# Graph attention on one core: 48 gathers added behind the batches, and one buffer for gathered rows less

## The chip, the cores and the metric

The kernel runs on one core of a Trainium2 chip. The metric is the device time of one execution in microseconds (us); the time before is the median of three runs. The profile is that of one execution of its own.

## What is computed

One graph-attention layer with a residual and a layer norm. There are N = 6250 nodes with D = 128 features, and E = 206250 edges, sorted by destination; 8 heads of 16 features each.

```python
Qh = (h @ WQ).reshape(N, H, D)
Kh = (h @ WK).reshape(N, H, D)
Vh = (h @ WV).reshape(N, H, D)
Eh = (edge_attr @ WE).reshape(-1, H, D)
src, dst = (edge_index[0], edge_index[1])
score = jnp.einsum('ehd,ehd,ehd->eh', Kh[src], Qh[dst], Eh) * inv_sqrt_d
score = jnp.exp(jnp.clip(score, -5.0, 5.0))
msg = Vh[src] * score[:, :, None]
wV = jax.ops.segment_sum(msg, dst, num_segments=N)
Z = jax.ops.segment_sum(score, dst, num_segments=N)
h_out = wV / (Z[:, :, None] + 1e-06)
x = layernorm(x + h_out)
```

## The kernel before

Edges are cut into 1612 tiles of 128, and the tiles into batches of four (smaller ones at the very end), about 405 in all. A table `kv` in DRAM holds the K and V rows of all nodes, 256 floats or 1 KB a node. The rows of an edge's source node are fetched by an indirect DMA on GpSimd's queue, the *gather* of line 314: 128 rows of 1 KB for each tile, four gathers for a batch, into one of GB = 17 buffers `kvrows` of 4 KB a partition. The first XB = 12 batches gather from `x`, since `kv` is still being written. The last tile has only 42 edges; its gather is cut to 64 rows.

The loop over batches is unrolled and in an order written out by hand. Step b does, in the order of the code: loads of edge features (`ea`), of relative destinations (`relb`) and of query windows (`qw`) on SyncE's queue; the four gathers of batch b (`gather(b)`); on TensorE the transposes of batch b-1 (`turn`, line 373, into `pps`), the expansion of the queries of batch b (`stage_a`, line 354, into `qps`) and its edge projection (line 358, into `eps`); the sums over finished windows of destinations (`finish`, line 401); on VectorE the product of batch b-2 with its gathered K rows (`stage_b`, line 379, `kq`) and its reduction (line 382), the messages of batch b-3 from its gathered V rows (`messages`, line 413), the one-hot matrices of batch b+2 (lines 340 and 344), and the product `eq` of batch b (line 365). ScalarE evicts `qps` (line 356), takes the exponentials (391, 393), and copies finished sums. TensorE adds up the messages by destination (`stage_c`, line 431, `agg`). Now and then `q_rows` (lines 258 to 265) makes another block of query rows: a matmul, a cast on ScalarE, a difference on VectorE, a cast and a difference again, and a store.

The gathers are tied to TensorE's pace. From batch LOCK = 16 on, the first gather of batch b waits for the matmul of line 354 of batch b - lag(b), where lag falls from 12 by one every four batches and is 1 from batch 60 on:

```python
def lag(b):
    return max(STEP, 12 - (b - LOCK) // 4)
```

A gather that takes a used buffer also waits until VectorE's line 413 has read the batch that had it.

The lines that the prediction uses: 314 (gathers), 354 (`qps`), 358 (`eps`), 365 (`eq`), 373 (`pps`), 379 (`kq`), 413 (`msg`), 431 (`agg`), 258, 261 and 262 (`q_rows`).

Of the kernel before, what the change touches and what calls it, by code (L numbers as in the profile page):

```python
# [8 lines left out]
F32 = mybir.dt.float32  # L9
# [6 lines left out]
P = 128  # L16
N, E, D, H, DH = 6250, 206250, 128, 8, 16
# [7 lines left out]
MW = D + H  # L25
B = 4
CH = 8
GB = 17
XB = 12
LOCK = XB + 4  # L30
STEP = 1
TAIL = 8
HEAD = 132
NG = (NT + G - 1) // G
# [14 lines left out]
def cut_batches():  # L49
    out, t = [], 0  # L50
    while t < NT:
        k = B
        if t >= NT - TAIL:
            k = 2 if NT - t > 3 else 1
        out.append(range(t, t + k))
        t += k
    return out
# [23 lines left out]
def edge_attention(ctx: ExitStack, tc: tile.TileContext, x, xT, srcT, dstT, dstB, dst0, bnd, lo, eaT,  # L81
                   wq, wkv, we, out, kv, qtab, qs, relD):
    nc = tc.nc
# [25 lines left out]
    def src_col(t):  # L109
        return src_sb[0][:, t:t + 1] if t < C0 else src_sb[1][:, t - C0:t - C0 + 1]  # L110

    with ExitStack() as fast:
        ip = fast.enter_context(tc.tile_pool(name="init", bufs=1))
        nc.scalar.dma_start(dst_sb[:, :C0], dstT[:, :C0])
        lo_sb = ip.tile([P, NG], I32, name="lo_sb")
        nc.scalar.dma_start(lo_sb, lo)
        io_i = ip.tile([P, 3 * P], I32, name="io_i")
# [84 lines left out]

        gp = fast.enter_context(tc.tile_pool(name="gather", bufs=GB))
        ep = fast.enter_context(tc.tile_pool(name="edges", bufs=EB))
# [42 lines left out]
        batches = cut_batches()  # L247
# [55 lines left out]
        def lag(b):  # L303

            return max(STEP, 12 - (b - LOCK) // 4)

        def gather(b):
            rows, f = (x, D) if b < XB else (kv, 2 * D)
            g = gp.tile([P, B, 2 * D], F32, name="kvrows")
            for i, t in enumerate(batches[b]):  # L310
                k = min(P, (E - t * P + 63) // 64 * 64)
                if k < P:
                    nc.vector.memset(g[k:, i, :], 0.0)
                ins = nc.gpsimd.indirect_dma_start(  # L314
                    out=g[:k, i, :f], out_offset=None, in_=rows,
                    in_offset=bass.IndirectOffsetOnAxis(ap=src_col(t)[:k], axis=0))
                if i == 0 and b >= LOCK:
                    tc.add_manual_dep(ins.ins, expanded[b - lag(b)].ins.name,
                                      mybir.DependencyInfo(mybir.DependencyClass.Sync, mybir.DependencyReason.DATA),
                                      reason="gathers keep to TensorE's pace")  # L320
            return g

        def project(g, n):
# [94 lines left out]
        def stage_c(b):  # L418
            n, g, oh, m = st8.pop(b)
            for i in range(n):  # L420
# [18 lines left out]
                elif last:  # L439
# [3 lines left out]
                    if k[1] == 0 and k[0] > 0:  # L443
                        ready.append(k[0] - 1)

        gathered = {b: gather(b) for b in range(min(XB, len(batches)))}
        for b0 in range(0, NB, KB):
            table(b0)
# [15 lines left out]
        for b in range(nbat + 4):  # L464
# [6 lines left out]
            if b < nbat:  # L471
                load_chunk(batches[b][0] // CH + EB - 3)
                load_rel(batches[b][0] // RC + 1)
                load_q(batches[b][0] // WT + QLOOK)
                g = gathered.pop(b) if b in gathered else gather(b)
                if b == min(XB, nbat - 1):
                    late_loads()
                if b == min(XB + 8, nbat - 1):
                    relative(C0, NT)
                if b == 14:  # L480
                    from_window(1)
                if b == 0:
                    for i in range(AHEAD):
                        stage_0(i)
                if b > 0:
                    turn(b - 1)
                stage_a(b, g)
            elif b == nbat:
                turn(b - 1)
# [178 lines left out]
```

## Time and profile before

| what | value |
|---|---|
| median of three runs | 2424.27 us (2415.33 to 2429.15) |
| the profiled execution | 2430.0 us, span 2428.1 us |
| mean granted TensorE clock | 0.81 |
| TensorE matmuls, busy | 1539.8 us, 63% |
| VectorE, busy | 1577.4 us, 65% |
| ScalarE, busy | 458.9 us, 19% |
| GpSimd, busy | 1534.0 us, 63% |
| DMA moved | 398.16 MB, mean 164 GB/s |
| gathers from `kv` | 1564, mean 951 ns on GpSimd |

How to read it: an engine's busy time counts its instructions and leaves out the time in which its sequencer issues, waits or branches. A gather's time on GpSimd is that of making its descriptors, not that of the transfer. Of each group of instructions a view gives the busy time, the mean time of one, and the idle time of the engine just before, with what ended it: "issue" stands where nothing that the profile shows was waited for, "remote" where the releaser is not among the instructions shown. In a timeline each line has the start, the length, the engine, the line of the code and the operation, and in brackets the idle time before it. The records of matmuls start when they are recorded to start, while their ends are modelled.

### The profile page before, as it was taken

Reading aid. Unit: us, or ns where it says so; the run is one execution under the profiler, and the core shown is the slowest. Engines: PE = TensorE matmul, PEld = TensorE weight load, DVE = VectorE, ACT = ScalarE, POOL = GpSimd, SP = SyncE. Lnnn points to the kernel's source line nnn. Section 1 sums busy time; section 2 is a strip of 40 time slices with the busy share of each in tenths; the row PEclk is TensorE's granted clock in tenths of the full one; section 3 lists DMA queues with packets and bytes.
Section 4 is the critical chain, followed back from the end, with each engine's and each line's share of the span. In section 5 each row is a group of like instructions: output and inputs, shape, how many; then the busy total and the mean of one; then the engine's idle time right before and its main releaser. Section 6 shows DMA issues by size and latency. Waiting matters only on the chain.

```text
span 2428.1 us, 24930 instructions
## 1 busy us (share of the span) xinstructions
PE 1539.8 (63%) x6880; PEld 1086.0 (45%) x6880; DVE 1577.4 (65%) x3779; ACT 458.9 (19%) x1572; POOL 1534.0 (63%) x1619
## 2 busy tenths in 40 slices
PE   3587666666665666657666666666666656656665
PEld 2365444444444444444444444444444444444444
DVE  1368778666766666667667666666666667666766
ACT  0232122111111111111111111111111111111111
POOL 7346565666666666666666666666666666666664
PEclk6898898887878888778877878788778788887887
DMA  5645555556554555556456554655555556554642
GB/s 176 201 144 174 179 156 178 165 150 185 170 166 148 168 177 156 164 152 196 147 157 196 160 156 149 184 168 151 169 162 178 147 155 196 157 156 146 197 150 71
DMA packets 178482, 398.16 MB, mean 164 GB/s; under 512 B 61756, under 2 KB 87526, under 8 KB 178336
## 3 DMA queue, kind: packets, MB, share of 16 engines
q0 software_dynamic: 76592, 208.18, 29.4%
q1 hardware_dynamic: 100604, 187.38, 25.2%
q8 instruction: 57, 0.93, 0.2%
q10 hardware_dynamic: 1140, 0.93, 0.1%
q14 instruction: 89, 0.73, 0.1%
HBM read 381.54 MB, written 14.81 MB: 163 GB/s over the span
## 4 chain that ended last, share of the span: by engine, by line
PE 34%; another core or an unknown queue 23%; DVE 19%; issue 16%; ACT 4%; DMA 2%; POOL 1%; DVEq 1%; SPq 0%; ACTq 0%; POOLq 0%
PE agg L431 10%; PE eps L358 10%; PE pps L373 7%; DVE sc L382 4%; DVE kq L379 4%; DVE eq L365 3%; PE qps L354 3%; ACT qT L356 2%; DVE msg L413 2%; PE finps L401 2%; POOL kvrows L314 1%; DVE onehot L340 1%; DVE onehotT L344 1%; DMA kvrows<-kv,src 1%
## 5 line engine op out<-in xcount | busy, mean ns | idle before, releaser
L314 POOL DMA_INDIRECT kvrows<-kv,src x1564 | 1487.1, 951 | 862.3 <-issue 385.6
L431 PEld LDWEIGHTS agg<-msg,onehot 128*128 128x128 f32 x3224 | 516.7, 230 | 664.3 <-issue 520.9
L431 PE MATMUL agg<-msg,onehot 128*128 128x136 f32 x3224 | 560.5, 326 | 352.8 <-DVE msg L413 137.2
L373 PE MATMUL pps<-shift,eq 128*128 128x128 f32 x1612 | 320.5, 332 | 419.6 <-DVE eq L365 238.5
L365 DVE TENSOR_TENSOR eq<-qT,eps 128x512 f32<-128x512 f32 x406 | 276.4, 681 | 476.2 <-ACT qT L356 210.9
L358 PE MATMUL eps<-ea,we_sb 128*128 128x512 f32 (+1 forms) x812 | 528.2, 738 | 16.8 <-issue 13.4
L373 PEld LDWEIGHTS pps<-shift,eq 128*128 128x128 f32 x1612 | 221.4, 168 | 477.4 <-DVE eq L365 282.4
L356 ACT COPY qT<-qps 128x512 f32<-128x512 f32 x406 | 236.8, 583 | 1048.5 <-remote 428.8
L379 DVE TENSOR_TENSOR kq<-kvrows,pps 128x512 f32<-128x512 f32 x406 | 274.8, 677 | 12.1 <-remote 3.5
L413 DVE TENSOR_TENSOR msg<-kvrows,bank 128x512 f32<-128x512 f32 x406 | 274.6, 676 | 9.8 <-ACT bank L391 4.3
L382 DVE TENSOR_REDUCE sc<-kq 128x32 f32<-128x512 f32 x406 | 276.0, 680 | 7.3
L340 DVE TENSOR_TENSOR onehot<-bank,dst_sb 128x512 f32<-128x512 f32 x406 | 275.8, 680 | 0.0
L358 PEld LDWEIGHTS eps<-ea,we_sb 128*128 128x128 f32 x812 | 192.1, 238 | 50.0 <-issue 14.6
L354 PE MATMUL qps<-onehotT,qw 126*128 126x512 bf16 x406 | 187.3, 461 | 0.9 <-ACT qT L356 0.9
L344 DVE TENSOR_SCALAR onehotT<-relb,node 126x512 bf16<-126x512 bf16 x406 | 147.0, 363 | 16.7 <-remote 11.2
L391 ACT ACTIVATE bank<-sc 128x32 f32<-128x32 f32 x406 | 83.0, 204 | 257.2 <-DVE onehot L340 139.8
L401 PEld LDWEIGHTS finps<-sum,shift 128*128 128x128 f32 x478 | 73.1, 215 | 62.4 <-issue 33.9
L401 PE MATMUL finps<-sum,shift 128*128 128x136 f32 x478 | 75.8, 307 | 30.9 <-ACT sum L441 26.2
L262 DVE TENSOR_TENSOR qr<-qrows,qst 128x128 f32<-128x128 f32 (+1 forms) x49 | 14.2, 289 | 116.8 <-ACT qst L261 104.4
L393 ACT ACTIVATE msg<-sc 128x32 f32<-128x32 f32 x406 | 88.0, 217 | 0.0
L385 DVE TENSOR_SCALAR sc<-sc 128x32 f32<-128x32 f32 x406 | 79.2, 195 | 7.3
L441 ACT COPY sum<-agg 128x136 f32<-128x136 f32 x146 | 39.3, 269 | 236.2 <-remote 100.7
(66 smaller groups left out, 525.9 us busy)
## 6 DMA issues: line engine op xcount, KB each, us to landing
ea<-eaT SPq DMA_DIRECT2D x201, 512.0 KB
relb<-relD SPq DMA_DIRECT2D x100, 504.0 KB
kvrows<-kv,src POOLq DMA_INDIRECT x1564
qw<-qs SPq DMA_DIRECT2D x202, 31.5 KB
kv<-kvst SPq DMA_DIRECT2D x12, 512.0 KB
qs<-qst SPq DMA_DIRECT2D x48, 96.0 KB
xb<-x SPq DMA_DIRECT2D x48, 64.0 KB
out<-h SPq DMA_DIRECT2D x48, 64.0 KB
```

What stands on the lines that cost most here:

```text
L314: ins = nc.gpsimd.indirect_dma_start(out=g[:k, i, :f], out_offset=None, in_=rows, in_offset=bass.IndirectOffsetOnAxis(ap=src_col(t)[:k], a ...
L340: nc.vector.tensor_tensor(oh[:, :n], iota_p[:, None, :].to_broadcast([P, n, P]), rel[:, t0:t0 + n, None].to_broadcast([P, n, P]), op=ALU.i ...
L354: expanded[b] = nc.tensor.matmul(pq[:, :n * P], loaded[t0 // WT], ohT[:, :n * P], start=True, stop=True)
L356: nc.scalar.copy(qT[:, :n * P], pq[:, :n * P])
L358: nc.tensor.matmul(pe[:, :n * P], we_sb, ea_tiles(t0, n), start=True, stop=True)
L365: nc.vector.tensor_tensor(eq[:, :n * P], qT[:, :n * P], pe[:, :n * P], op=ALU.mult)
L373: nc.tensor.transpose(pp[:, i, :], eq[:, i * P:i * P + P], ident)
L379: nc.vector.tensor_tensor(t1[:, :n], g[:, :n, :D], pp[:, :n], op=ALU.mult)
L382: nc.vector.tensor_reduce(sc[:, :n], t1[:, :n].rearrange("p b (h d) -> p b h d", h=H), axis=AX.X, op=ALU.add)
L401: nc.tensor.matmul(ps, shift[:, P - s:2 * P - s], sums[k], start=i == 0, stop=stop and i == len(parts) - 1)
L413: nc.vector.tensor_tensor(m[:, :n, :D].rearrange("p b (h d) -> p b h d", h=H), g[:, :n, D:].rearrange("p b (h d) -> p b h d", h=H), exp_p[ ...
L431: nc.tensor.matmul(aggs[k], oh[:, i, :], m[:, i, :], start=first and not final, stop=last)
```

## The change

Behind the gathers of each batch from 100 to 147 one more gather is issued on GpSimd's queue. It reads rows of `kv` by the first r indices of the batch's first tile, with r from a list of twelve values, each used in four batches running: 124, 126, 127, 120, 112, 96, 64, 32, 16, 8, 4, 2. All 48 write the first r partitions of one tile `short` (1 KB a partition), which nothing reads. The buffers for gathered rows become 16 instead of 17, which makes room for that tile.

```diff
-GB = 17
+GB = 16
...
+SHORT = [r for r in (124, 126, 127, 120, 112, 96, 64, 32, 16, 8, 4, 2) for _ in range(4)]
...
         ip = fast.enter_context(tc.tile_pool(name="init", bufs=1))
         nc.scalar.dma_start(dst_sb[:, :C0], dstT[:, :C0])
+        short = ip.tile([P, 2 * D], F32, name="short")
...
                                       reason="gathers keep to TensorE's pace")
+            for r in SHORT[b - 100:b - 99] if b >= 100 else ():
+                nc.gpsimd.indirect_dma_start(
+                    out=short[:r], out_offset=None, in_=kv,
+                    in_offset=bass.IndirectOffsetOnAxis(ap=src_col(batches[b][0])[:r], axis=0))
             return g
```

## The prediction

> **What bounds the kernel now.** I read the page's busy shares first, then its costliest groups, then the answers on line 314 (the gathers): what they wait for, their timeline, and the stretch in which the change acts.
>
> ```profile
> PE 1539.8 (63%) x6880; PEld 1086.0 (45%) x6880; DVE 1577.4 (65%) x3779; ACT 458.9 (19%) x1572; POOL 1534.0 (63%) x1619
> ...
> L314 POOL DMA_INDIRECT kvrows<-kv,src x1564 | 1487.1, 951 | 862.3 <-issue 385.6
> ```
>
> No engine is full: TensorE (PE), VectorE (DVE) and GpSimd (POOL) stand at 63 to 65%. But busy time leaves out the issue time between two gathers. The answer on line 314 has it:
>
> ```profile
> L314 POOL DMA_INDIRECT kvrows<-kv,src x1564: 901/949/1403, 96.2 to 2412.2; - x196
> ...
>   issue: 399.9, 1306
>   remote: 221.7, 110
> ...
>   POOL kvrows L314: 5.0, 11
> ```
>
> Of the 1564 gathers, 1306 came after idle time with nothing to wait for ("issue"), 399.9 / 1306 = 0.306 us each. A gather thus occupies GpSimd for 0.949 + 0.306 = 1.255 us, a batch of four for 5.02 us. All 1564 make 1963 us, 81% of the 2428.1 us span. The last line says that gathers waited for an earlier gather's landing 11 times, 5.0 us together: landing is no limit today. The timeline around 745 us shows what the rest is:
>
> ```profile
> 739.77 0.38 PE L258 MATMUL qrows<-wq_sb,xT_sb 128*128 128x128 f32 x2
> ...
> 743.97 0.95 POOL L314 DMA_INDIRECT kvrows<-kv,src  x1 [0.30 <-issue]
> 745.23 0.94 POOL L314 DMA_INDIRECT kvrows<-kv,src  x1 [0.30 <-issue]
> 747.06 0.27 ACT L261 CAST qst<-qrows 128x128 bf16<-128x128 f32 x1 [7.33 <-remote]
> 747.36 0.29 DVE L262 TENSOR_TENSOR qr<-qrows,qst 128x128 f32<-128x128 f32 x1 [6.52 <-issue]
> ...
> 748.78 0.95 POOL L314 DMA_INDIRECT kvrows<-kv,src  x1 [2.61 <-remote]
> ```
>
> The matmul of line 258 is recorded at 739.77, yet ScalarE (ACT) can read its result only at 747.06, after the run of gathers ended at 746.17. TensorE, ScalarE and VectorE all stand still in between, and only GpSimd works. GpSimd then pauses 2.61 us, until TensorE has passed the expansion of the batch before (line 354), and everybody goes on. This repeats all along: counted over the gather timeline behind batch 25, 159 idle times exceed 0.7 us, 136 of them lie between 1.8 and 2.8 us, and the runs between them are 12 gathers long 93 times, 8 long 33 times, 4 long 30 times. The pause is about as long after a short run as after a long one. The other engines do a batch in about 3.6 us in their bursts (differences of the starts of line 379), and then wait until GpSimd has issued what it has in hand. I cannot name what holds TensorE's result back. But a pause of fixed length behind a run of any length means that GpSimd waits for a consequence of its own last gather, not for an independent clock. So GpSimd's chain sets the pace: n gathers at 1.255 us, plus a pause.
>
> **The stretch.** Batches 100 to 147 issue their gathers from 644.6 to about 922 us.
>
> ```profile
> 644.50:921.00 276.50, 181.14 (x191) 0.81 0.58 170
> ```
>
> (Columns: length, GpSimd's busy time and gathers, granted clock, DMA share, GB/s.) Idle is 276.5 - 181.1 = 95.4 us; 191 x 0.302 = 57.7 us of it are the ordinary 0.30 us between gathers, 37.7 us are pauses, 0.79 us a batch. A batch takes 276.5 / 47.75 = 5.79 us.
>
> **The added gathers.** The row counts are four each of 124, 126, 127, 120, 112, 96, 64, 32, 16, 8, 4 and 2, mean 831 / 12 = 69.25. What GpSimd pays for fewer rows shows once: the last tile's gather has 64 rows and took 0.901 us (the minimum above, the last gather in the timeline), 0.048 us less than one of 128. In a line through both, 69.25 rows take 0.905 us. With 0.302 us ahead of it a gather costs 1.207 us, and 48 cost 57.9 us. The bounds: if time went with rows, 0.949 x 69.25 / 128 + 0.302 = 0.815 us and 39 us in all; if each took the longest gather's time, 1.403 + 0.302 = 1.705 us and 82 us. I take 57.9, since 64 rows were measured and this lies next to it.
>
> Where it lies: behind the four gathers of its batch, on the same in-order queue, so the next batch's gathers and with them the pause and the release of TensorE move back by it. By the chain above nothing covers it. If the 37.7 us of pauses were real slack they would cover that much, and 57.9 - 37.7 = 20.2 us would be left.
>
> More pauses are the bound above. TensorE makes three batches in 11 us whatever GpSimd does; with 6.2 us a batch on GpSimd it overtakes earlier. With a pause of 2.0 us above the ordinary gap in every batch, in place of 0.79, 48 x 1.21 = 58 us would come on top. I take none, since the 12-long runs already hold three batches of 5.02 us against bursts of 3.6.
>
> **The added waits.** All added gathers write one tile, so each may wait for the landing of the one a batch before; behind it on GpSimd stand all later gathers, and behind them VectorE's product of line 379. It was issued over 6 us earlier, and a gather's wait for a landing was at most 1.9 us, 11 times in 1564 (the waits of GpSimd). So 0 at the least, 48 x 1.9 = 91 us at the most. I take 0, the row's frequency being 0.7%.
>
> A rule speaks against that zero. The Trainium skill, "DMA: Bandwidth & Descriptors", in its section on why a DMA increments its semaphore by 16, says that a transfer goes over the largest number of engines, up to 16, that divides its row count: 127 rows go over one engine, 126 over 14, 124 over 4, and it knows of exceptions among direct copies issued from GpSimd. By the page the four gathers of 127 rows would each put 32 packets on one engine. No run here shows such a row count. Here a packet took on average 0.294 x 16 x 2428 / 76592 = 0.149 us, over all sizes, from this line:
>
> ```profile
> q0 software_dynamic: 76592, 208.18, 29.4%
> ```
>
> By 208.18 MB in 11,420 us of engine time, 127 KB would then take 7.1 us on one engine, the next added gather would wait some 2 us, and four such waits would add about 8 us to the sum.
>
> The bytes are no matter: 48 x 69.25 KB is 3.4 MB beside 398 MB.
>
> **One buffer less.** A gather now reuses the buffer of 16 batches before instead of 17. Its product of line 413 belongs to three steps behind that batch, while the gather anyway waits for the expansion of at most 12 batches before (one before, from batch 60 on), which TensorE's order puts later. So no wait is added: 0. If that cover failed, the first reuse alone would wait, one batch or 5.8 us.
>
> **Sum.** 57.9 us. The profiled execution took 2430.0 us (span 2428.1) and would take 2487.9; the median of the runs, 2424.27, lies 5.7 us lower and gives 2482.
>
> **Rivals.** (a) GpSimd has slack, and the result is not slower. If the others' chain set the 5.79 us a batch, the pauses would swallow 37.7 us, and the remaining 20.2 us would draw down the lead of the gathers over line 379: its start lies 13 us (median) behind its first gather's, though the last row landed only 6 us before. Batches from 148 on refill the lead. Then 20 - 6 = 14 us at most are left, near 0 if the lead before goes deeper: 2424 to 2438. For it: GpSimd 63% busy, pauses put down to other engines. Against it: the constant pause, and everyone else idle during the long runs. It decides if pauses in the stretch vanish. (b) The pauses swallow 37.7 us and the lead gives nothing: 2445. (c) Odd row counts are slow to land or to issue, or each batch gets its pause: between 66 and 116 us more, 2490 to 2540. (d) The unread gathers are dropped on the way to the chip: no change; the tile is written by a DMA, which nothing in the code marks as removable. (e) Added waits break up the long runs and release TensorE earlier, so that pauses shrink by more than the gathers cost. They hold only 37.7 us in the stretch, so a gain needs cheap gathers too.
>
> **How the numbers follow.** The full price, from about 39 to 82 us, has 0.55; (c) beyond it 0.15; (b) 0.15; (a) and (d) 0.11; (e) 0.04. Half a per cent, 12 us, is about what a measurement of this kernel can tell from no change. Slower by more takes the first three and a part of (a), 0.87; same 0.09, faster 0.04. The range runs from (b) less a little, 2441, to the top of (c), 2540.
>
> **What would show it.** Right: 48 more gathers near 0.90 us on GpSimd; in the stretch batches of 6.9 to 7.0 us, runs of 5, 10 or 15 gathers, pauses that add up to about 38 us still; outside it the same pace as before. Wrong, towards (a): pauses nearly gone between the added gathers and batches of 6.2 us or less. Towards (c): idle time before the added gathers put down to a DMA, largest around the 127-row ones, or gathers that take over 1 us.

## The result, and the profile after

The changed kernel takes 2507.8 us (median of three runs, 2506.2 to 2510.6) against 2424.27 us: a ratio of 1.035, 95% interval 1.033 to 1.037, so 83.5 us more. The profiled execution has a span of 2504.4 us, 76.3 us more. Lines below `gather` have moved: 314 is now 316, the added gathers are line 324, 354 is 360, 356 is 362, 379 is 385.

The busy shares and the costliest group of the page, as before:

```profile
PE 1553.7 (62%) x6880; PEld 1094.9 (44%) x6880; DVE 1579.2 (63%) x3779; ACT 459.0 (18%) x1572; POOL 1587.1 (63%) x1667
...
L316 POOL DMA_INDIRECT kvrows<-kv,src x1564 | 1488.3, 952 | 849.8 <-issue 390.9
```

GpSimd (POOL) has 48 operations and 53.1 us of busy time more, yet its share stays 63%: the span grew along. The ordinary gathers cost what they did (952 ns). The stretch of batches 100 to 147, all engines (length; busy time and instructions of PE, PEld, DVE, ACT and POOL; granted clock, DMA share, GB/s), and then the answer on the added gathers:

```profile
639.50:1004.60 365.10, 189.86 (x798) 136.46 (x797) 185.04 (x440) 50.63 (x178) 235.02 (x240) 0.74 0.48 139
```

```profile
L324 POOL DMA_INDIRECT short<-kv,src x48: 856/912/2564, 644.7 to 1001.5; - x48
...
  issue: 14.9, 41
  DMA short<-kv,src: 13.7, 4
```

The stretch took 278.3 us before and takes 365.0, 86.7 more; all of the change is in it. The rest of the kernel runs at its old pace or a little faster (5.81 us a batch behind batch 148, 5.84 before); over the whole span this is 10 us, less than the 13.8 us by which the three runs of the kernel before differ. The median added gather takes 0.912 us, but the longest 2.564, and four waits for the landing of an earlier added gather make 13.7 us. Three of these four are in this part of GpSimd's timeline, its added gathers alone:

```profile
694.70 0.98 POOL L324 DMA_INDIRECT short<-kv,src  x1 [0.30 <-issue]
...
702.91 2.56 POOL L324 DMA_INDIRECT short<-kv,src  x1 [2.19 <-issue]
...
714.39 2.55 POOL L324 DMA_INDIRECT short<-kv,src  x1 [3.90 <-DVE eq L371]
...
725.14 2.55 POOL L324 DMA_INDIRECT short<-kv,src  x1 [3.17 <-DMA short<-kv,src]
...
736.27 2.55 POOL L324 DMA_INDIRECT short<-kv,src  x1 [3.52 <-DMA short<-kv,src]
...
749.90 0.99 POOL L324 DMA_INDIRECT short<-kv,src  x1 [6.05 <-DMA short<-kv,src]
```

These are the last gather of 126 rows, the four of 127 and the first of 120. Only the 127s take 2.55 us, and GpSimd stands idle for 2.2 to 6.1 us ahead of them and of the one behind them. The first of these waits comes behind a gather of 126 rows, the other four behind a 127, and the next added gather starts 10.7 to 13.6 us after the 127 did. The profile puts two of the five down to something else than the landing; the kernels with one and with four tiles below decide that. These batches take 9.8 to 12.1 us. The four gathers of 124 rows take 1.30 us; the other forty 0.86 to 1.00 us, whether they have 2 rows (0.87) or 126 (0.98).

The pause behind a run is there as before (GpSimd, ScalarE and VectorE around 683 us):

```profile
679.28 0.99 POOL L324 DMA_INDIRECT short<-kv,src  x1 [0.30 <-issue]
683.08 0.59 ACT L362 COPY qT<-qps 128x512 f32<-128x512 f32 x1 [5.38 <-remote]
683.32 0.98 POOL L316 DMA_INDIRECT kvrows<-kv,src  x1 [3.05 <-remote]
...
683.70 0.69 DVE L371 TENSOR_TENSOR eq<-qT,eps 128x512 f32<-128x512 f32 x1 [9.06 <-ACT qT L362]
```

ScalarE waited 5.4 us and VectorE 9.1 us; GpSimd came to its wait last and left it with them.

### The profile page after: what moved, and what is told of

It reads as the page before. It is cut to its first block, busy times and chain, and to the rows that moved or that the text cites. A ratio compares the mean times of both kernels' runs of the same rounds, so it can differ in the third digit from the quotient of the medians.

```text
span 2504.4 us, 25025 instructions
## 1 busy us (share of the span) xinstructions
PE 1553.7 (62%) x6880; PEld 1094.9 (44%) x6880; DVE 1579.2 (63%) x3779; ACT 459.0 (18%) x1572; POOL 1587.1 (63%) x1667
## 4 chain that ended last, share of the span: by engine, by line
PE 29%; another core or an unknown queue 24%; DVE 21%; issue 16%; ACT 4%; DMA 3%; POOL 2%; DVEq 0%; ACTq 0%; SPq 0%; POOLq 0%
PE eps L364 9%; PE agg L437 8%; PE pps L379 6%; DVE sc L388 4%; DVE kq L385 4%; DVE eq L371 3%; DVE msg L419 3%; PE qps L360 2%; DVE onehot L346 2%; ACT qT L362 2%; POOL kvrows L316 2%; PE finps L407 1%; DVE onehotT L350 1%; DMA short<-kv,src 1%
## 5 line engine op out<-in xcount | busy, mean ns | idle before, releaser
L364 PE MATMUL eps<-ea,we_sb 128*128 128x512 f32 (+1 forms) x812 | 534.7, 747 | 14.9 <-ACT kvrows L341 10.7
L350 DVE TENSOR_SCALAR onehotT<-relb,node 126x512 bf16<-126x512 bf16 x406 | 146.6, 362 | 18.1 <-remote 11.3
L610 DVE TENSOR_SCALAR rz<-fin 128x8 f32<-128x8 f32 x48 | 8.9, 185 | 120.4 <-ACT fin L414 73.0
```

Of the source, the lines that this page charges most:

```text
L364: nc.tensor.matmul(pe[:, :n * P], we_sb, ea_tiles(t0, n), start=True, stop=True)
```

## The experiments

Each kernel ran beside the kernel before on the same chip. The chips differ: on two of them the kernel before took 2043.6 us (the first four kernels) and 2043.2 us (the last four), on a third 2425.2 us (the four in between), about what it took where the change was measured. I call them the 2.04 ms chips and the 2.42 ms chip. Each was met in one round of runs only, so that the difference lies in the chip itself, and not in something else of that round, is not shown. This matters, as will be seen.

**128 rows in all 48.**

```diff
-SHORT = [r for r in (124, 126, 127, 120, 112, 96, 64, 32, 16, 8, 4, 2) for _ in range(4)]
+SHORT = [128] * 48
```

> All 48 added gathers have 128 rows. Theory (GpSimd's own time is the pace, odd row counts cost extra): 48 x (0.949 + 0.305) = 60 us more than before, no waits ahead of the added gathers, batches of 7.0 us in the stretch. Rival 'slack' (the pauses are free time and cover first): 60 - 38 = 22 us more. Rival 'row counts are no matter' (the 83 us of the change come from the number of gathers alone): 80 us or more again.

On a 2.04 ms chip: 2109.0 against 2043.6, ratio 1.032 [1.030, 1.033], 65 us more. **2 rows in all 48:**

```diff
+SHORT = [2] * 48
```

> All 48 added gathers have 2 rows, 2 KB instead of 128 KB. Theory: 48 x (0.87 + 0.305) = 56 us more than before, within 5 us of the run with 128 rows, as nearly all of a gather's time on GpSimd is fixed. Rival 'bytes' (what is moved and its landing sets the price): close to 0. Rival 'slack': 56 - 38 = 18 us.

2107.8, ratio 1.031 [1.029, 1.032], 64 us more. A 64th of the bytes saves 1 us, so "bytes" falls. Both fit GpSimd's own time, 48 x 1.25 and 48 x 1.18 us, and 7 and 6 us of idle time ahead of the added gathers, where no wait was expected. They say nothing against the slack: on this chip GpSimd has no pauses that could cover anything, as the kernel with the buffers alone will show.

For the 2.42 ms chip the change's own trace has a part of the answer. Its last twelve batches, with added gathers of 8, 4 and 2 rows and far behind the 127s, take 7.47 us each, 1.67 us more than the 5.80 before, though GpSimd's own time there is 6.2 us a batch. So there, too, the price is not that of the bytes.

**The 127s replaced by 128s.**

```diff
-SHORT = [r for r in (124, 126, 127, 120, 112, 96, 64, 32, 16, 8, 4, 2) for _ in range(4)]
+SHORT = [r for r in (124, 126, 128, 120, 112, 96, 64, 32, 16, 8, 4, 2) for _ in range(4)]
```

> The change with 128 rows in place of the four 127s, else unchanged. Theory: the 127-row gathers cost 4 x 1.6 us more on GpSimd and some 17 us of waits for their landing, so about 22 us less than the change: 61 us more than before. Rival 'waits stand in for pauses' (the waits only replace pauses that would come anyway): about 76 us more than before, only the 6 us on GpSimd are saved.

2110.4, ratio 1.033 [1.031, 1.035], 67 us more. That is as little as with 128 rows throughout. On this chip the change itself was not run, so the saving cannot be read off here; what 127 rows cost was measured with the kernels of all 127s below.

**The buffers alone.**

```diff
+SHORT = []
```

> 16 buffers instead of 17 and the tile short allocated, but no gather added. Theory: no difference from before, under 0.3%. Rival 'buffers' (the part of the 83 us that the gathers' time on GpSimd, 66 us, leaves open comes from here): 15 to 20 us more.

2043.6 against 2043.6, ratio 0.9996 [0.9987, 1.0005]. The buffer is free, as predicted. (The iota kernel below, with 16 buffers too, shows no loss on the 2.42 ms chip either.) Since this program is the kernel before but for the buffer, its trace also shows how that kernel runs on a 2.04 ms chip. GpSimd's timeline there, and the stretch of batches 100 to 147 (all engines):

```profile
602.45 0.94 POOL L316 DMA_INDIRECT kvrows<-kv,src  x1 [0.30 <-issue]
603.70 0.94 POOL L316 DMA_INDIRECT kvrows<-kv,src  x1 [0.30 <-issue]
604.95 0.94 POOL L316 DMA_INDIRECT kvrows<-kv,src  x1 [0.30 <-issue]
```

```profile
509.90:750.30 240.40, 165.00 (x799) 116.84 (x800) 187.93 (x448) 53.18 (x180) 181.87 (x193) 0.88 0.64 192
```

GpSimd never pauses: from batch 100 on no idle time over 0.7 us is left, and a batch takes 5.01 us = 4 x 1.253. The gathers cost the same there as on the 2.42 ms chip (0.946 us median). What is missing are the pauses, and the matmul results that come late: "ACT qT <- remote" has no line there. In the waits of before it is the second longest:

```profile
ACT qT L356 <- remote: 428.8, 89, 8.9
```

TensorE's granted clock alone does not tell the chips apart. It is 0.88 in this stretch and 0.82 in that of before; but with 128 rows in all 48 it is 0.80 on the same 2.04 ms chip, and yet the batch takes 6.41 us there, next to GpSimd's own 6.26.

**127 rows in all 48**, on the 2.42 ms chip.

```diff
+SHORT = [127] * 48
```

> All 48 added gathers have 127 rows and write one tile. Theory (127 rows go over one DMA engine: slow to issue and slow to land, and the next one waits for the landing): batches of about 11 us in the stretch as around the four of the change, 48 x (11.2 - 5.8) = 260 us more than before. Rival 'only issue is slow': 48 x (2.55 + 0.305) = 137 us. Rival 'the cost of the four was chance': 60 us.

2687.3 against 2425.2, ratio 1.109 [1.106, 1.113], 262 us more. **The same into four tiles in turn**, on the same chip:

```diff
-        short = ip.tile([P, 2 * D], F32, name="short")
+        shorts = [ip.tile([P, 2 * D], F32, name=f"short{i}") for i in range(4)]
...
-                    out=short[:r], out_offset=None, in_=kv,
+                    out=shorts[b % 4][:r], out_offset=None, in_=kv,
```

> As the run before, but the 127-row gathers write four tiles in turn, so that each waits for the one four batches earlier. Theory (the wait on the one tile costs the part above 137 us): the waits ahead of the added gathers go, and 137 us more than before are left, up to 175 if the pauses grow. Rival 'landing holds the queue whatever the tile' (the one engine or the semaphores are the limit): as with one tile, about 260 us.

2529.5, ratio 1.043 [1.040, 1.046], 104 us more. So the wait for the one tile costs 158 of the 262 us. The answers on the added gathers, first with one tile, then with four:

```profile
L324 POOL DMA_INDIRECT short<-kv,src x48: 2542/2547/2558, 652.2 to 1187.5; - x48
...
  DMA short<-kv,src: 139.4, 40
```

```profile
L324 POOL DMA_INDIRECT short<-kv,src x48: 2544/2548/2560, 653.5 to 1028.3; - x48
...
  issue: 14.3, 47
```

Issue stays slow, the waits go. With four tiles the price is 104 us and not the 137 expected: GpSimd's pauses of the stretch, 37.3 us before, shrink to 4.8, and 137 - 33 = 104. Here the pauses did pay. That the 127 rows go over one DMA engine can be read from the packets, though the trace does not number the engines. The line of the page's part 2, before and with 127s:

```profile
DMA packets 178482, 398.16 MB, mean 164 GB/s; under 512 B 61756, under 2 KB 87526, under 8 KB 178336
```

```profile
DMA packets 203826, 404.77 MB, mean 160 GB/s; under 512 B 85564, under 2 KB 111334, under 8 KB 203680
```

23808 small packets more are 496 for each added gather. By the sizes in the trace they are 16 of 4 bytes, as every gather has, 465 of 16 and 15 of 12 bytes; the data are 31 packets of 4096 bytes and one of 3072, which is 127 rows in one sequence. 465 + 15 = 480 = 15 x 32: as many as fifteen other engines with 32 small packets each make. The change's own trace agrees over all twelve row counts. If each gather goes over the largest number of engines, up to 16, that divides its rows, and each engine moves its rows in packets of up to four, the 48 gathers need 660 packets of 4096 bytes, 84 of 3072, 128 of 2048 and 176 of 1024; its software queue has just these numbers more than before.

**An iota instead of a gather**, on the 2.42 ms chip.

```diff
-        short = ip.tile([P, 2 * D], F32, name="short")
+        short = ip.tile([P, 960], I32, name="short")
...
-            for r in SHORT[b - 100:b - 99] if b >= 100 else ():
-                nc.gpsimd.indirect_dma_start(
-                    out=short[:r], out_offset=None, in_=kv,
-                    in_offset=bass.IndirectOffsetOnAxis(ap=src_col(batches[b][0])[:r], axis=0))
+            if 100 <= b < 148:
+                nc.gpsimd.iota(short, pattern=[[1, 960]], base=0, channel_multiplier=0)
```

> In place of each added gather GpSimd makes an iota of 128 x 960, some 0.93 us by the line through the iotas of 384 and 128 columns (0.443 and 0.226 us); no DMA, no descriptors. Theory (occupied GpSimd time is the price, whatever it does): 48 x (0.93 + 0.05 to 0.3) = 47 to 59 us more than before. Rival 'the DMA is the price' (descriptors, queues, transfers): close to 0. Rival 'slack': 10 to 20 us.

2425.0 against 2425.2, ratio 0.9994 [0.998, 1.001]: nothing. My theory of GpSimd's occupied time falls on this chip, and so does its reading of the pauses. The iotas took 0.947 us each, next to a gather's time; the stretch is 280.9 us against 278.3, with GpSimd busy all through, and pauses of 0.6 us in all. GpSimd's timeline, and the waits of the stretch:

```profile
701.43 0.95 POOL L316 DMA_INDIRECT kvrows<-kv,src  x1 [0.30 <-issue]
702.39 0.94 POOL L324 IOTA short<- 128x960 int32 x1
703.49 0.95 POOL L316 DMA_INDIRECT kvrows<-kv,src  x1 [0.16 <-DVE onehotT L348]
704.75 0.95 POOL L316 DMA_INDIRECT kvrows<-kv,src  x1 [0.30 <-issue]
```


```profile
ACT qT L360 <- PE qps L358: 70.3, 39, 3.5
DVE kq L383 <- DMA kvrows<-kv,src: 58.9, 25, 6.4
...
ACT qT L360 <- remote: 5.1, 1, 5.1
```

And the first line of the waits of before, from 644.5 to 921 us:

```profile
ACT qT L356 <- remote: 64.8, 14, 8.9
```

An iota has no idle time ahead of it and only 0.16 us behind it, so a batch grows by 0.83 us beside 4 x 1.255. That makes 40 us, and the pauses held 37.3: by the slack, 3 us of the stretch would be left, and 2.5 were measured. With the iotas the late matmul results are nearly gone (5.1 us; 64.8 us in as long a stretch before), and VectorE now waits for gathered rows. So the pauses were time that GpSimd had, and other work filled it. "The DMA is the price" fits as well: an operation without a DMA cost nothing.

**Another tie to TensorE**, on the 2.42 ms chip (the kernel before otherwise).

```diff
-STEP = 1
+STEP = 2
```

> The kernel before, with the gathers of batch b tied to the expansion of batch b-2 instead of b-1 from batch 56 on (STEP = 2); nothing is left out. Theory (GpSimd's chain: gathers at 1.255 us and a pause of about 2 us behind each run that waits for its own consequence): the pauses go or become rare, up to 0.7 us a batch over 340 batches, so 100 to 240 us less than before. Rival 'TensorE is released only when GpSimd pauses' (the pause is what lets the others go on, whatever is waited for): no gain, the other engines stand still until something else stops GpSimd, same time or slower. Rival 'another engine's pace': no difference.

2421.1, ratio 0.998 [0.997, 1.000]. The gathers now run ahead of line 379 by 18.5 us instead of 12.9 (medians behind batch 148), and still pause as often and as long: behind batch 148, 100 pauses of 2.5 us, before 99. The 100 to 240 us of my theory fall: the gathers run a batch further ahead, and no pause goes. Both rivals expected no gain, and this run does not part them.

The last four kernels were to tell whether gathers alone, or any DMA of GpSimd, have that price on the 2.42 ms chip. They met a 2.04 ms chip, where GpSimd's own time explains most of what they took, and so left this open. **A plain DMA instead of the added gather:**

```diff
+            if 100 <= b < 148:
+                nc.gpsimd.dma_start(short, kv[:P])
```

> In place of each added gather GpSimd's queue issues a plain DMA of the first 128 rows of kv into the same tile. Two theories of why an added gather costs its full price and an iota of the same length nothing, both for a chip on which the kernel before takes 2.42 ms (5.8 us a batch, 1.45 us a gather). 'Rate' (something behind GpSimd takes 1.45 us for each of its DMAs, whatever it moves): 48 x 1.45 = 70 us more, and the pauses stay. 'Indirect' (it is the indirect descriptors only): 0 to 20 us more, and the pauses shrink as with the iota. On a chip on which the kernel before takes 2.04 ms GpSimd never pauses, and its own time counts: 48 x 1 to 1.3, 48 to 62 us more by both.

2084.2, ratio 1.020 [1.018, 1.022], 41 us more, less than the 48 to 62 expected: it takes 0.586 us on GpSimd, 28 us for all 48, and 8 us of idle time stand ahead of five of them. **One gather less in the 48 batches:**

```diff
+                if 100 <= b < 148 and i == 3:
+                    nc.sync.dma_start(g[:, i, :], kv[:P])
+                    continue
                 ins = nc.gpsimd.indirect_dma_start(
```

> The kernel before with one gather less in batches 100 to 147: the fourth tile's rows are loaded from SyncE's queue as the first 128 rows of kv, so these tiles compute with other rows than the reference's. 'Rate' or GpSimd's own time (the number of gathers sets the pace): 48 x 1.45 = 70 us less where the kernel before takes 2.42 ms, 48 x 1.25 = 60 us less where it takes 2.04 ms, in both as long as the other engines keep up (they made a batch in 3.6 us in bursts). Rival 'another engine's chain sets the 5.8 us a batch and GpSimd only waits for it': no difference.

1988.3, ratio 0.973 [0.971, 0.975], 55 us less: a batch of the stretch takes 3.86 us, near 3 x 1.253 = 3.76, where 60 us less were expected. **2 rows once more** (the edit as above):

> All 48 added gathers with 2 rows once more. Where the kernel before takes 2.42 ms: 'rate' 70 us more, with pauses left in the stretch, though GpSimd's own time is 5.02 + 1.17 = 6.2 us a batch; 'slack' (as the iota had it) 48 x (6.2 - 5.8) = 19 us more without pauses. Where it takes 2.04 ms: 64 us more again.

2107.6, ratio 1.031 [1.030, 1.033], 64 us more again, as expected. **The iota once more** (the edit as above):

> The iota in place of each added gather once more. Where the kernel before takes 2.42 ms: no difference, as GpSimd's pauses of 0.8 us a batch cover it. Where it takes 2.04 ms and GpSimd never pauses: 48 x 0.85 to 0.95 = 41 to 46 us more.

2083.3, ratio 1.019 [1.018, 1.021], 40 us more. The same iota that is free on the 2.42 ms chip costs 48 x 0.83 us here; its stretch takes 280.1 us, on the 2.42 ms chip 280.9. With the iotas GpSimd is the limit on both.

## Why the prediction was right

**Time on GpSimd**, predicted 57.9 us: measured 66.5 us, namely 51.9 us of gathers and 48 x 0.305 us ahead of them. Forty of the 48 cost nearly what the line through 64 and 128 rows gives for them (mean 0.911 us, by the line 0.897). The four 127s took 2.55 us, the 124s 1.30 us, together 7.9 us more than the line.

**Waits for the one tile**, predicted 0: measured 21.2 us ahead of the added gathers, 17.3 of it at the four 127s and the gather behind them: 1.9 at the first, which waits for the last 126, and 15.4 behind the 127s. The step that was wrong is the choice of the zero from a row of ordinary gathers. The rule of the Trainium skill that was set against it, "DMA: Bandwidth & Descriptors", in its section on why a DMA increments its semaphore by 16, on the number of engines that divides the row count, fits these gathers: their packets have the sizes that rows so divided make, 127 rows in one sequence. The prediction's estimate with it, 8 us for four waits, was half of what they took; it left out that a 127 already takes 2.55 us to issue. The kernels with one and with four tiles show the wait as the cause.

**Pauses**, predicted to stay at 37.7 us: 37.3 us before, 35.7 after. **The buffer**, predicted 0: 0. So 66.5 + 21.2 - 1.6 = 86.1 of the 86.7 us of the stretch are accounted for. The sum of 57.9 us is short by the waits and the odd row counts, some 29 us. This is the first half of rival (c), with the signs that the prediction gave for it: gathers of over 1 us, and idle time put down to a DMA around the 127s. It came on top of the full price.

**The reason** was only half right, and that the sum came near is in part luck. The prediction said that GpSimd's own chain sets the pace and that a pause is a consequence of its last gather, so that anything put on GpSimd costs its full time. On the 2.04 ms chips that is so: no pauses, 4 x 1.253 us a batch, iotas cost what they occupy, gathers and plain DMAs that and 6 to 8 us of waits, and a gather less saves 55 of 60 us. On the 2.42 ms chip, the one that the prediction was for, it is not: the iota cost nothing, and the pauses were the slack that rival (a) took them for. Yet the added gathers did not get that slack. Behind the 127s, batches 112 to 147 take 7.21 us on average without the 5.7 us that the first of them waits for the landing of a 127, while GpSimd's own work there is some 6.2 us. So the pauses stayed at the predicted size, but not for the predicted reason: they are neither a fixed cost behind every run, as the iotas show, nor free for whatever GpSimd does.

What fits all stretches of the 2.42 ms chip in which GpSimd pauses is a price for each gather, added or not: before 278.3 / 192 = 1.45 us, with STEP = 2 1.45, after the change (365.0 - 21.2) / 240 = 1.43, where the waits for the one tile are taken off (1.49 in its last twelve batches). With the iotas GpSimd's own 1.46 us for each gather is as much, so they are free; with the 127s in four tiles its own 7.88 us a batch is more than 5 x 1.45, the pauses vanish, and the batch takes 7.97. By this the change should cost 48 x 1.45 + 21 = 91 us, against 87 in the stretch. This is a reading after the fact and not shown: STEP = 2 is nearly the kernel before, so that only the change itself tests the price, and the run that would have tried it, one gather less, met a 2.04 ms chip. Another reading is left, too: the iota may help not because it is no gather, but because it breaks up the run of gathers. What holds the matmul results back on the one chip and not on the others, and why more gathers mean more of it, stays open.

## What to carry to other kernels

A pause in front of a queue can be slack for one kind of work and not for another: on the 2.42 ms chip an iota of 0.95 us went into GpSimd's pauses for nothing, while a gather of the same length, with 0.3 us ahead of it, cost its full price. To tell whether a pause is slack, put an operation of the same length and another kind in the place. And mind the row count and the target of an indirect DMA: 48 gathers of 127 rows into one tile cost 262 us, into four tiles 104 us.

## What was not expected of the hardware

- Row counts: an indirect gather of 2 to 112 rows takes 0.86 to 0.94 us on GpSimd, of 120, 126 or 128 rows 0.95 to 0.99 us, of 124 rows 1.30 us, of 127 rows 2.55 us. A gather of 127 rows brings 480 more packets of 12 or 16 bytes, and with one target tile the batches take 11.3 us.
- Chips: the same kernel took 2425 us on one chip and 2043 us on two others, 16% less, with the same time for each gather (0.95 us). Of the 386 us between the spans of before and of the buffers alone, 318 are GpSimd's pauses behind batch 25 (159 idle times over 0.7 us, 367.0 us, less 0.305 us each), which the faster chips do not show, and 32 us lie ahead of the first gather from `kv` (it starts at 96.2 and 64.2 us). Why is open.
